# A selective scan whose tiles hold 64 channels x 2 states instead of 128 channels x 1 state

## The chip, the cores and the metric

The kernel runs on one NeuronCore of a Trainium2 chip. The metric is the device time of one execution in microseconds (us); lower is better. TensorE is called PE in the profile, VectorE DVE, ScalarE ACT, GpSimd POOL, and SP is the engine that issues most of the DMAs.

## The reference, cut to what matters

Eight images of 64 channels x 64 x 64 positions go through four layers: a self-attention over 4096 positions, two window-attention blocks with an MLP, a filter layer, and a state-space layer (SS2D) with an output stage. The change lies in the scan of the last one. It has B = 8 images, K = 4 directions, 128 channels c, N = 16 states n, and 4096 positions in a row:

```
def step(h, inp):
    u_t, dt_t, B_t, C_t = inp
    h = h * exp(dt_t[..., None] * A) + dt_t[..., None] * B_t[:, :, None, :] * u_t[..., None]
    return (h, einsum('bkcn,bkn->bkc', h, C_t))
```

So for each image, direction, channel and state there is a first-order recurrence along the positions, h = exp(dt*A[c,n])*h + (dt*u)[c]*B[n], and the output y[c] is the sum over the 16 states of h*C[n]. B and C depend on the state and the position, not on the channel; dt and u depend on the channel and not on the state; A depends on both.

## The kernel before, in words

**Frame.** The images are worked on in four pairs. First a head runs with PE alone in charge: all layers up to the scan's inputs for the first pair, and the first layer for the second. Then `scans` runs for pair after pair, 512 steps each, and feeds other work in beside the steps from generators: the front of the next pair (`front`: the attention of `layer0`, the window blocks of `layer1`, `layer2`, `scan_sources`) and the back of the pair before (`back`). The loop at the end of each step advances the generators in a fixed proportion to the steps done, so the amount of other work per step is fixed by their costs. Beside the last pair there is only back work. A second, general program at the end of the kernel is entered only when values run out of range; it isn't touched.

**A unit** is one image, one direction and one chunk of 512 positions: 64 units per pair, 256 in all. `inputs` (called one unit ahead, after the second step) loads the unit's x tile (L1703), makes dt in PSUM with a matmul (L1706), Exp and Ln on ACT (L1708, L1711), then writes dt*x (L1712, DVE) and dt (L1713, ACT) to the tile `du`. A second matmul (L1715) gives the 16 rows of B and 16 of C, ACT copies them (L1717), and SP stores them to DRAM as `rows` (L1719).

**A step** takes two of the 16 states; eight steps make a unit. `fetch` (L1726, SP) loads two rows of B, three steps ahead, and two of C, two steps ahead, each row spread over all 128 partitions: a tile of 128 x 2 x 512 floats. B and C have three buffers each. `products` (L1731, POOL, two steps ahead) makes v = B * (dt*x) for both states in one instruction; v has six buffers. `step` then does for each state j: Exp(dt*A) on ACT into a PSUM bank `dad` (L1753), the scan on DVE (L1756) into `hd` or in place into `dad`, a small ACT copy of the last column to `carry` (L1764), and the product with C. The number `own` says how many of the two states have that product on DVE (L1771) rather than on POOL (L1767 for both states at once, L1771 for one).

**The sum over states.** `sums` runs one step late: per state one matmul of v with a 128 x 128 identity (L1795) that accumulates in the PSUM bank `yd`. At the unit's end DVE adds `yd` to `Y` (L1805 to L1810).

**The dense stretches.** While `layer0` runs beside the scan it sets `dense` to 1. Then `own` is one higher, the products that DVE makes are not given to PE but added up by DVE in the tile `ysum` (L1774, L1776, L1777), and `ysum` goes through PE once per unit.

**Order.** Every engine runs its instructions in one static order. A scheduler of the language makes it from the program's order and dependencies and may interleave scan and other work; `net.behind` (in `sums`) ties a sum behind the product of the next step. All B and C loads, the x loads and the stores of `rows` sit in SP's one queue, which stops at the first DMA whose wait isn't met. PSUM has three banks for `dad`, `pdd` and `pbc` (tag da), one for `yd`, three for the other work and one for its totals.

Of the kernel before, what the change touches and what calls it, by code (L numbers as in the profile page):

```python
# [9 lines left out]
F32 = mybir.dt.float32  # L10
AF = mybir.ActivationFunctionType
ALU = mybir.AluOpType
# [3 lines left out]
B, C, HH, WW = 8, 64, 64, 64  # L16
L = HH * WW
P = 128
# [5 lines left out]
DI, NST, RNK, KDIR = 128, 16, 4, 4  # L24
TD = 512
# [63 lines left out]
def _pack(w):  # L89
    items = []  # L90

    def put(name, a):
        a = np.asarray(a, np.float32)
        shape = a.shape
        flat = a.reshape(shape[0], -1)
        if shape[0] < P:
            flat = np.concatenate([flat, np.zeros((P - shape[0], flat.shape[1]), np.float32)], axis=0)
        items.append((name, shape, flat))

    eye = np.eye(64, dtype=np.float32)  # L100
# [5 lines left out]
    f = {k[len("L0_conv_"):]: v for k, v in w.items() if k.startswith("L0_conv_")}  # L106
# [7 lines left out]
    f = {k[len("L1_conv_"):]: v for k, v in w.items() if k.startswith("L1_conv_")}  # L114
# [36 lines left out]
    f = {k[len("L2_conv_"):]: v for k, v in w.items() if k.startswith("L2_conv_")}  # L151
# [29 lines left out]
    f = {k[len("L3_conv_"):]: v for k, v in w.items() if k.startswith("L3_conv_")}  # L181
# [11 lines left out]
    put("xbc", xp[:, RNK:].transpose(2, 0, 1))  # L193
    put("xr", xp[:, :RNK].transpose(1, 0, 2))
    put("drT", f["dtproj_w"].transpose(2, 0, 1))
    put("alogs", f["A_logs"].reshape(KDIR, DI, NST).transpose(1, 0, 2))
    dtT = f["dtproj_w"].transpose(2, 0, 1)
    put("dtT", np.concatenate([np.zeros((2 * NST,) + dtT.shape[1:], np.float32), dtT], axis=0))
    put("dtb", f["dtproj_b"].T)
# [8 lines left out]
    for i in range(4):  # L208
        s = slice(16 * i, 16 * i + 16)
# [948 lines left out]
class _Direct:  # L1158
# [112 lines left out]
    def layer0(self, p):  # L1271
# [11 lines left out]
        with self.work("w0") as wk:  # L1283
# [40 lines left out]
            self.dense = 0  # L1324
            sums = net.sums[:, p]
            nc.vector.tensor_reduce(sums, parts, AX.X, ALU.add)
            rec = wk.tile([P, 2, 32], F32, name="rec", tag="rec", bufs=1)
            nc.vector.reciprocal(rec, sums)
# [368 lines left out]
    def inputs(self, u):  # L1697

        nc, w, net = self.nc, self.w, self.net
        wk, ps = self.sw, self.ps  # L1700
        k, c = u["k"], u["c"]
        x = u["x"] = wk.tile([P, TD], F32, name="xs", tag="xs")
        nc.sync.dma_start(x, self.kept[u["image"]][k % 2][:, c * TD : (c + 1) * TD])  # L1703

        pd = ps.tile([P, TD], F32, name="pdd", tag="da")
        nc.tensor.matmul(pd, lhsT=net.xdt[:, k, :], rhs=x, start=True, stop=True)  # L1706
        du = u["du"] = wk.tile([P, 2, TD], F32, name="du", tag="du")
        nc.scalar.activation(  # L1708
            pd, pd, AF.Exp, bias=w["dtb"][:, k : k + 1], accum_out=net.esum[:, u["image"], k, c : c + 1]
        )  # L1710
        nc.scalar.activation(pd, pd, AF.Ln, bias=1.0)  # L1711
        nc.vector.tensor_tensor(du[:, 1], pd, x, ALU.mult)  # L1712
        nc.scalar.activation(du[:, 0], pd, AF.Copy)  # L1713
        pb = ps.tile([2 * NST, TD], F32, name="pbc", tag="da")
        nc.tensor.matmul(pb, lhsT=w["xbc"][:, k, :], rhs=x, start=True, stop=True)  # L1715
        bc = wk.tile([2 * NST, TD], F32, name="bc", tag="bc")
        nc.scalar.activation(bc, pb, AF.Copy)  # L1717
        rows = u["rows"] = self.dram.tile([2 * NST, TD], F32, name="rows", tag="rows")
        nc.sync.dma_start(rows, bc)  # L1719

    def fetch(self, i, st, s):

        n = NST * s + 2 * (i % 8)
        t = st["BC"[s]] = self.sw.tile([P, 2, TD], F32, name="BC"[s], tag="BC"[s], bufs=3)
        row = self.units[i // 8]["rows"][n : n + 2].rearrange("r t -> (r t)")
        self.nc.sync.dma_start(t.rearrange("p r t -> p (r t)"), row.unsqueeze(0).to_broadcast([P, 2 * TD]))  # L1726

    def products(self, i, st):
        v = st["v"] = self.sw.tile([P, 2, TD], F32, name="vd", tag="v", bufs=6)
        dx = self.units[i // 8]["du"][:, 1:2]  # L1730
        self.nc.gpsimd.tensor_tensor(v, st["B"], dx.to_broadcast([P, 2, TD]), ALU.mult)  # L1731

    def step(self, i, st):

        nc, w, net = self.nc, self.w, self.net
        wk, ps = self.sw, self.ps
        u = self.units[i // 8]
        k, c, at, CC, v = u["k"], u["c"], u["at"], st["C"], st["v"]


        n0 = 2 * (i % 8)
        own = 1 + (i % 4 == 3) if u["image"] >= B - 2 else i % 2 + self.dense
        rev = k >= 2

        def along(t):
            return t[:, ::-1] if rev else t

        h = wk.tile([P, 2 - i % 2, TD], F32, name="hd", tag=f"h{i % 2}", bufs=1)
        hs = []
        for j in range(2):  # L1750
            n = n0 + j
            da = self.bank("dad", (P, TD), "da")
            nc.scalar.activation(da, u["du"][:, 0], AF.Exp, scale=net.As[:, k, n : n + 1])  # L1753
            first = 0.0 if at == 0 else self.carries[:, n : n + 1]
            to = da if j >= 2 - own else h[:, j]
            nc.vector.tensor_tensor_scan(along(to), along(da), along(v[:, j]), first, ALU.mult, ALU.add)  # L1756
            hs.append(to)
            if at < NTD - 1 and (own or j):
                ends = h[:, :, 0] if rev else h[:, :, TD - 1]
                cs = self.carries[:, n0 : n0 + 2]  # L1760
                if own:
                    ends = to[:, 0:1] if rev else to[:, TD - 1 : TD]
                    cs = self.carries[:, n : n + 1]
                nc.scalar.activation(cs, ends, AF.Copy)  # L1764

        if own == 0:
            st["w"] = nc.gpsimd.tensor_tensor(v, h, CC, ALU.mult)  # L1767
        for j in range(2 if own else 0):
            if j < 2 - own or not self.dense:
                engine = nc.vector if j >= 2 - own else nc.gpsimd  # L1770
                m = engine.tensor_tensor(v[:, j], hs[j], CC[:, j], ALU.mult)  # L1771
            elif "sum" not in u:
                s = u["sum"] = wk.tile([P, TD], F32, name="ysum", tag="ysum", bufs=1)
                m = nc.vector.tensor_tensor(s, hs[j], CC[:, j], ALU.mult)  # L1774
            else:
                m = nc.vector.tensor_tensor(hs[j], hs[j], CC[:, j], ALU.mult)  # L1776
                nc.vector.tensor_tensor(u["sum"], u["sum"], hs[j], ALU.add)  # L1777
            st.setdefault("w", m)
        st["to_y"] = [v[:, j] for j in range(2) if not self.dense or j < 2 - own]
        if i % 8 == 7 and "sum" in u:  # L1780
            st["to_y"].append(u["sum"])

    def sums(self, i, st, after=None):

        nc, w, net = self.nc, self.w, self.net
        wk, ps = self.sw, self.ps
        u = self.units[i // 8]
        k, c = u["k"], u["c"]
        srcs = st["to_y"]
        for j, v in enumerate(srcs):  # L1790
            start = "y" not in u
            if start:
                u["y"] = ps.tile([P, TD], F32, name="yd", tag="y", bufs=1)
            stop = i % 8 == 7 and j == len(srcs) - 1
            m = nc.tensor.matmul(u["y"], lhsT=w["ident"], rhs=v, start=start, stop=stop)  # L1795
            if after is not None and j == 0:
                net.behind(m, after)
        if i % 8 < 7:
            return

        y = u["y"]
        yd = net.part(self.Y, k, c)
        yp = y.rearrange("p (a b) -> p a b", b=64)
        if u["nth"] == 0:
            nc.vector.scalar_tensor_tensor(yd, self.img(u["x"]), net.dsum, yp, ALU.mult, ALU.add)  # L1805
        elif u["nth"] < 3:
            nc.vector.tensor_tensor(yd, yd, yp, ALU.add)
        else:
            o = u["x"]
            nc.vector.tensor_tensor(self.img(o), yd, yp, ALU.add)  # L1810
            nc.sync.dma_start(u["out"][:, c * TD : (c + 1) * TD], o)
# [155 lines left out]
```

## Time and profile before

| | us |
|---|---|
| median of 3 runs (13437.7 to 13443.52) | 13439.18 |
| span of the profiled execution | 13435.7 |
| of it before the first product of the scan | 2189 |
| PE busy | 10771.7 (80%) |
| DVE busy | 8806.3 (66%) |
| POOL busy | 7764.7 (58%) |
| ACT busy | 7082.9 (53%) |
| DMA: bytes moved, mean rate | 2385 MB, 178 GB/s |

The span is the time from the first to the last instruction of one profiled execution; the runs are separate, unprofiled executions. Busy times of engines overlap, so they don't add up to the span. In a group's line the columns are: source line, engine, operation, output<-inputs, shapes, count; then busy time and mean duration in ns; then idle time of the engine just before these instructions and what ended it. Each float32 matmul of the program shows as two records of PE. In the table by stage each row gives a stretch of time, its length, and for each engine the busy time and (in brackets) the number of instructions.

### The profile page before, as it was taken

How to read it: one execution, taken by the hardware profiler on the slowest of the kernel's cores; microseconds unless marked ns; L12 is line 12 of the kernel's file. 1: busy time of each engine (PE TensorE's matmuls, PEld its weight loads, DVE VectorE, ACT ScalarE, POOL GpSimd, SP SyncE). 2: the span in 40 equal slices, each digit the busy share in tenths (PEclk: the TensorE clock that was granted, in tenths of full speed). 3: DMA queues.
4: the chain of work that ended last, by engine and by line, in shares of the span. 5: the costliest groups of instructions: out<-in, count | busy, mean ns of one | idle time of the engine just before them, and what ended most of it. 6: DMA issues, size and time to landing. Idle time of an engine off the chain costs nothing. (4 is left out here: it accounts for less than half of the span.)

```text
span 13435.7 us, 140355 instructions
## 1 busy us (share of the span) xinstructions
PE 10771.7 (80%) x45762; PEld 3974.5 (30%) x45762; DVE 8806.3 (66%) x10407; ACT 7082.9 (53%) x15569; POOL 7764.7 (58%) x3875
## 2 busy tenths in 40 slices
PE   9999986888787669989888666997898766666676
PEld 2243322333232222224433222223443222222222
DVE  0121236777768676676666767667676767987987
ACT  5556514565535646655554644664654554454553
POOL 0000004888778765466666686446766677787883
PEclk9999977998898789989899788998989878888888
DMA  0000004666667765455555675445545577677884
GB/s 24 1 1 1 1 14 166 233 236 218 212 213 239 237 206 170 161 182 173 172 177 175 224 241 177 157 161 179 192 170 170 195 239 260 233 281 263 293 297 156
DMA packets 706250, 2385.13 MB, mean 178 GB/s; under 512 B 81120, under 2 KB 81248, under 8 KB 704480
## 3 DMA queue, kind: packets, MB, share of 16 engines
q1 hardware_dynamic: 681312, 2319.76, 51.0%
q10 hardware_dynamic: 24192, 56.29, 1.1%
q8 instruction: 362, 5.93, 0.2%
q14 instruction: 384, 3.15, 0.1%
HBM read 2272.97 MB, written 102.76 MB: 177 GB/s over the span
## 5 line engine op out<-in xcount | busy, mean ns | idle before, releaser
L1731 POOL TENSOR_TENSOR vd<-B,du 128x1024 f32<-128x1024 f32 x2048 | 4832.8, 2367 | 3958.5 <-DMA B<-rows 2538.2
L1795 PE MATMUL yd<-vd,pack 128*128 128x512 f32 x7540 | 4300.3, 701 | 1351.0 <-POOL vd L1767 585.1
L1753 ACT ACTIVATE dad<-du,As 128x512 f32<-128x512 f32 x4096 | 2729.4, 681 | 1136.3 <-DVE hd L1756 686.4
L1756 DVE TENSOR_TENSOR_SCAN hd<-dad,carry,vd 128x512 f32<-128x512 f32 x2166 | 2714.5, 1270 | 683.9 <-ACT dad L1753 392.9
L1795 PEld LDWEIGHTS yd<-vd,pack 128*128 128x128 f32 x7540 | 1509.5, 217 | 3824.9 <-issue 1678.9
L1767 POOL TENSOR_TENSOR vd<-hd,C 128x1024 f32<-128x1024 f32 x658 | 1551.0, 2357 | 1050.5 <-DVE hd L1756 690.5
L1756 DVE TENSOR_TENSOR_SCAN dad<-dad,carry,vd 128x512 f32<-128x512 f32 x1418 | 1791.8, 1275 | 118.9 <-ACT dad L1753 64.8
L1771 POOL TENSOR_TENSOR vd<-hd,C 128x512 f32<-128x512 f32 x1154 | 1477.9, 1281 | 522.0 <-DVE hd L1756 474.3
L1313 ACT ACTIVATE e<-s 128x512 f32<-128x512 f32 x2048 | 1200.8, 591 | 750.3 <-PE s L1307 748.7
L1307 PE MATMUL s<-X 64*128 64x512 f32 x4096 | 1343.9, 646 | 30.5 <-ACT e L1313 28.8
L1299 PE MATMUL po<-e,VT 128*64 128x512 f32 x4096 | 1227.0, 621 | 12.6 <-ACT e L1313 9.9
L1771 DVE TENSOR_TENSOR vd<-dad,C 128x512 f32<-128x512 f32 x1300 | 866.0, 673 | 67.1 <-ACT carry L1764 46.8
L1764 ACT ACTIVATE carry<-hd 128x1 f32<-128x1 f32 (+1 forms) x1586 | 316.8, 201 | 908.0 <-DVE hd L1756 904.9
L1764 ACT ACTIVATE carry<-dad 128x1 f32<-128x1 f32 x1422 | 240.5, 169 | 786.5 <-DVE dad L1756 783.6
L1307 PEld LDWEIGHTS s<-X 64*128 64x128 f32 x4096 | 375.6, 186 | 914.9 <-issue 782.8
L1447 DVE TENSOR_TENSOR w_e<-w_s,bias 128x512 f32<-128x512 f32 x512 | 330.0, 681 | 426.9 <-PE w_s L1435 426.3
L1462 PEld LDWEIGHTS w_av<-vals,w_e 64*64 64x64 f32 x16384 | 538.9, 143 | 195.4 <-issue 84.2
L1462 PE MATMUL w_av<-vals,w_e 64*64 64x9 f32 x16384 | 567.1, 206 | 32.0 <-ACT w_e L1452 31.8
L1706 PE MATMUL pdd<-xs,xdt 128*128 128x512 f32 x512 | 343.0, 757 | 236.8 <-DMA xs<-xc 102.8
L1452 ACT ACTIVATE w_e<-w_e 128x512 f32<-128x512 f32 x512 | 311.9, 626 | 367.7 <-DVE w_e L1447 250.6
L1299 PEld LDWEIGHTS po<-e,VT 128*64 128x64 f32 x4096 | 236.3, 135 | 847.2 <-issue 763.6
L1574 PE MATMUL acc<-tap,pack 128*128 128x512 f32 x576 | 367.1, 761 | 98.2 <-DVE tap L1573 96.8
(252 smaller groups left out, 11102.0 us busy)
## 6 DMA issues: line engine op xcount, KB each, us to landing
B<-rows SPq DMA_DIRECT2D x2048, 512.0 KB, 5.1
C<-rows SPq DMA_DIRECT2D x2048, 512.0 KB, 4.5
xs<-xt SPq DMA_DIRECT2D x128, 256.0 KB, 3.6
xs<-xc SPq DMA_DIRECT2D x128, 256.0 KB, 4.2
xc<-xcv ACTq DMA_DIRECT2D x64, 256.0 KB, 3.9
zs<-z ACTq DMA_DIRECT2D x64, 256.0 KB, 3.8
xt<-XT ACTq DMA_DIRECT2D x32, 512.0 KB, 7.9
rows<-bc SPq DMA_DIRECT2D x256, 64.0 KB, 1.6
```

Source lines behind the costliest of these rows:

```text
L1299: nc.tensor.matmul(po[half[im]], lhsT=VT[:, t, half[im]], rhs=es[im], start=(t == 0), stop=(t == 31))
L1307: nc.tensor.matmul(ss[im], lhsT=at(half[im], t), rhs=X[half[im], jc * CH : (jc + 1) * CH], start=True, stop=True)
L1313: nc.scalar.activation(e, ss[im], AF.Exp, scale=C**-0.5, accum_out=parts[:, im, t, jc : jc + 1])
L1462: nc.tensor.matmul(self.av[half[im], x % 4 + j, h, :], lhsT=es[h // 4][half[im], j, h % 4, :], rhs=V[half[im], x + j, h, :], start=True, s ...
L1574: nc.tensor.matmul(acc, lhsT=w["ident"], rhs=tap, start=(t == 0), stop=(t == TAPS - 1))
L1731: self.nc.gpsimd.tensor_tensor(v, st["B"], dx.to_broadcast([P, 2, TD]), ALU.mult)
L1753: nc.scalar.activation(da, u["du"][:, 0], AF.Exp, scale=net.As[:, k, n : n + 1])
L1756: nc.vector.tensor_tensor_scan(along(to), along(da), along(v[:, j]), first, ALU.mult, ALU.add)
L1764: nc.scalar.activation(cs, ends, AF.Copy)
L1767: st["w"] = nc.gpsimd.tensor_tensor(v, h, CC, ALU.mult)
L1771: m = engine.tensor_tensor(v[:, j], hs[j], CC[:, j], ALU.mult)
L1795: m = nc.tensor.matmul(u["y"], lhsT=w["ident"], rhs=v, start=start, stop=stop)
```

## The change

The tile of one scan instruction holds 64 channels x 2 states on its 128 partitions (partition 2c + s is channel c, state s of the pair), where it held 128 channels x 1 state. Per step there are still two scan tiles; the index j now means the half of the channels, and not the state.

- B and C: a load writes two rows alternately to the partitions, 128 x 512 floats (256 KB in place of 512 KB). Both halves of the channels read the same tile. The buffers are four each.
- dt and dt*x: computed as before, into a tile `du1` (one buffer). Two DMAs per unit on SP (512 KB each, SBUF to SBUF) write every channel's two rows to two neighbouring partitions of `du`, one DMA per half of the channels. Exp and the products read `du`.
- The sums: per half one matmul with `fold`, a 128 x 64 matrix with two ones in each column, so that it adds the two states of a channel; half 0 goes to partitions 0 to 63 of `yd`, half 1 to partitions 64 to 127.
- `ysum` and its DVE additions are gone; in the dense stretches all 16 tiles of a unit go through PE. `own` is as before.
- The table of A is laid out to match. The rows' copy `bc` has one buffer in place of two.

```diff
-        du = u["du"] = wk.tile([P, 2, TD], F32, name="du", tag="du")
+        one = wk.tile([P, 2, TD], F32, name="du1", tag="du1", bufs=1)
+        du = u["du"] = wk.tile([P, 2, 2, TD], F32, name="du", tag="du")
...
-        nc.vector.tensor_tensor(du[:, 1], pd, x, ALU.mult)
-        nc.scalar.activation(du[:, 0], pd, AF.Copy)
+        nc.vector.tensor_tensor(one[:, 1], pd, x, ALU.mult)
+        nc.scalar.activation(one[:, 0], pd, AF.Copy)
+        for g in range(2):
+            src = one[self.HALF[g]].rearrange("c q t -> c (q t)").unsqueeze(1).to_broadcast([64, 2, 2 * TD])
+            nc.sync.dma_start(du[:, g].rearrange("p q t -> p (q t)"), src)
...
-        bc = wk.tile([2 * NST, TD], F32, name="bc", tag="bc")
+        bc = wk.tile([2 * NST, TD], F32, name="bc", tag="bc", bufs=1)
...
-        t = st["BC"[s]] = self.sw.tile([P, 2, TD], F32, name="BC"[s], tag="BC"[s], bufs=3)
-        row = self.units[i // 8]["rows"][n : n + 2].rearrange("r t -> (r t)")
-        self.nc.sync.dma_start(t.rearrange("p r t -> p (r t)"), row.unsqueeze(0).to_broadcast([P, 2 * TD]))
+        t = st["BC"[s]] = self.sw.tile([P, TD], F32, name="BC"[s], tag="BC"[s], bufs=4)
+        row = self.units[i // 8]["rows"][n : n + 2]
+        self.nc.sync.dma_start(t, row.unsqueeze(0).to_broadcast([64, 2, TD]))
...
-        self.nc.gpsimd.tensor_tensor(v, st["B"], dx.to_broadcast([P, 2, TD]), ALU.mult)
+        self.nc.gpsimd.tensor_tensor(v, self.twice(st["B"]), self.units[i // 8]["du"][:, :, 1], ALU.mult)
...
-            nc.scalar.activation(da, u["du"][:, 0], AF.Exp, scale=net.As[:, k, n : n + 1])
+            nc.scalar.activation(da, u["du"][:, j, 0], AF.Exp, scale=net.As[:, k, n : n + 1])
...
-            if j < 2 - own or not self.dense:
-                engine = nc.vector if j >= 2 - own else nc.gpsimd
-                m = engine.tensor_tensor(v[:, j], hs[j], CC[:, j], ALU.mult)
-            elif "sum" not in u:
-                s = u["sum"] = wk.tile([P, TD], F32, name="ysum", tag="ysum", bufs=1)
-                m = nc.vector.tensor_tensor(s, hs[j], CC[:, j], ALU.mult)
-            else:
-                m = nc.vector.tensor_tensor(hs[j], hs[j], CC[:, j], ALU.mult)
-                nc.vector.tensor_tensor(u["sum"], u["sum"], hs[j], ALU.add)
+            engine = nc.vector if j >= 2 - own else nc.gpsimd
+            m = engine.tensor_tensor(v[:, j], hs[j], CC, ALU.mult)
...
-            m = nc.tensor.matmul(u["y"], lhsT=w["ident"], rhs=v, start=start, stop=stop)
+        for j in range(2):
+            m = nc.tensor.matmul(
+                u["y"][self.HALF[j]], lhsT=w["fold"], rhs=st["v"][:, j], start=(i % 8 == 0), stop=(i % 8 == 7)
+            )
```

## The prediction

> **What bounds it now.** First the slices of the page.
>
> ```profile
> PE   9999986888787669989888666997898766666676
> POOL 0000004888778765466666686446766677787883
> PEclk9999977998898789989899788998989878888888
> DMA  0000004666667765455555675445545577677884
> ```
>
> No engine is full throughout. After the head (6 slices, no scan, not touched) the limit moves, so I cut the scan at its stages and read the table of busy time (columns: stretch, its length, PE, weight loads, DVE, ACT, POOL, clock, DMA share, GB/s).
>
> ```profile
> 2189.00:3076.00 887.00, 728.70 (x4929) 324.08 (x4929) 664.28 (x754) 511.73 (x1027) 783.19 (x383) 0.92 0.70 236
> 3076.00:4236.00 1160.00, 947.91 (x3683) 376.68 (x3681) 818.60 (x907) 556.33 (x1133) 921.69 (x449) 0.90 0.64 216
> 5070.00:5880.00 810.00, 774.29 (x2368) 211.13 (x2367) 525.63 (x619) 536.62 (x1549) 365.35 (x183) 0.98 0.49 164
> 5880.00:7412.00 1532.00, 1293.03 (x8031) 579.18 (x8030) 1065.86 (x1313) 791.81 (x1525) 1006.80 (x489) 0.89 0.53 178
> 7412.00:8270.00 858.00, 547.46 (x882) 186.01 (x882) 639.79 (x690) 428.88 (x786) 618.97 (x297) 0.77 0.64 218
> 11171.00:13436.00 2265.00, 1507.36 (x2618) 499.84 (x2618) 1950.98 (x2142) 1081.97 (x2425) 1676.18 (x896) 0.85 0.74 256
> ```
>
> With the steps counted by L1731 in each: A (first row) 192 steps of 4.62 us, POOL 88%; B 224 of 5.18, PE 82%, POOL 79%; D (dense) 119 of 6.8, PE 96%; E 245 of 6.25, PE 84%; F 149 of 5.76, no engine above 75%; G (last pair) 512 of 4.42, DVE 86%. D, E and F return for the third pair (119, 245 and 97 steps); 4236 to 5070 (C, 149 steps of 5.6) is like F. POOL works about 4.1 us per step in A to F outside D.
>
> Then the groups and who keeps POOL waiting.
>
> ```profile
> L1731 POOL TENSOR_TENSOR vd<-B,du 128x1024 f32<-128x1024 f32 x2048 | 4832.8, 2367 | 3958.5 <-DMA B<-rows 2538.2
> L1795 PE MATMUL yd<-vd,pack 128*128 128x512 f32 x7540 | 4300.3, 701 | 1351.0 <-POOL vd L1767 585.1
> L1299 PE MATMUL po<-e,VT 128*64 128x512 f32 x4096 | 1227.0, 621 | 12.6 <-ACT e L1313 9.9
> ```
>
> ```profile
> POOL vd L1731 <- DMA B<-rows: 2538.2, 227, 2172.5
> POOL vd L1731 <- PE yd L1795: 769.3, 181, 19.0
> ```
>
> The sums cost PE 4300 us. POOL waits 769 us until a late sum frees a buffer of v. Of the wait for B, 2172.5 is the head; 366 us is left.
>
> **The skill.** (1) "TensorE: Matmul & The Clock Gate", section "Part 3: Packing small matmuls — row/col tiling": matmuls in different column groups run at once. The trace agrees: attention's L1299 has the shape of the new sums (128 rows, 64 columns, two halves of one bank), and a pair costs 1227.0/1024 = 1.20 us busy against 4300.3/3770 = 1.14 for one full matmul. (2) "TensorEngine Tiling (Array Packing)", "Key Properties": a change of tiling mode drains the engine. In the dense stretch a pair, a full matmul and the next pair start 1.01 and 1.05 us apart, so I take 1.20 per pair with drains in it.
>
> ```profile
> 5530.97 1.08 PE L1299 MATMUL po<-e,VT 128*64 128x512 f32 x4
> 5531.98 1.13 PE L1795 MATMUL yd<-vd,pack 128*128 128x512 f32 x2
> 5533.03 1.13 PE L1307 MATMUL s<-X 64*128 64x512 f32 x4
> ```
>
> (3) The first of these pages, "Part 1: The HAM clock gate": an idle PE falls to half its clock. The table agrees: 0.77 in F with PE at 64%, 0.98 in D. A relieved PE will be slower per matmul. (4) "SBUF — State Buffer", "Door 1: The DMA port swizzle": 64 partitions reach half of the ports. The DMAs of du read 64; no run here shows its price yet.
>
> **Part by part.**
>
> *Sums outside D.* Two matmuls (2 x 1.12 in E) become a pair of 1.20. The built order of PE has both halves adjacent for 65% of the pairs in E, about 90% in B and A, nearly all in F and G; I count a split pair at the price of two. E: 551 us of sums become 245 x (0.65 x 1.20 + 0.35 x 2.24) = 383, so 168 less. B: 485 become 292, 193 less. A: 408 become 257. What reaches the end? From A to B to E, PE work per step grows 3.80, 4.23, 5.28 and the step 4.62, 5.18, 6.25: about 1 us per us. But other work grows with it, and split stages wait on DVE and ACT too, so I take 0.6 in E: -101, twice: -202. B has POOL's floor near, A's 4.62 per step: 0.5, -97. A is on that floor: -20.
> C and both F (395 steps) hold about 1 us of PE relief per step, which nothing there is short of; 0.15 for shorter waits: -55. G is DVE's: 512 x 1.1 x 0.1 = -56, with B's waits in it.
>
> *D, the dense stretches.* PE did 88 full matmuls (176 records, 96.5 us) in 119 steps; it will do 119 pairs x 1.20 = 143. PE is the bound, so +46, twice: +92. The 100 us per stretch of ysum additions that DVE loses are hidden behind PE and bring nothing. If PE had slack the +92 would vanish.
>
> *B and C.* 4096 loads halve. The floor is the 256 KB row.
>
> ```profile
> B<-rows SPq DMA_DIRECT2D x2048, 512.0 KB, 5.1
> xs<-xt SPq DMA_DIRECT2D x128, 256.0 KB, 3.6
> ```
>
> So B lands about 1.5 us sooner; only the 366 us of waits can gain, and they are counted in the shares above. The fourth buffer takes a wait from SP (fetches wait on POOL and DVE there), with the same cover.
>
> *du.* 512 more DMAs of 512 KB on SP, 268 MB against 1074 MB saved. In SP's built order they stand right after the store of rows, ahead of the next unit's first B, and wait for the DVE product and the ACT copy. In the timelines of all units that pair ends 2.2 us (median) after bc, then two issues of 0.35. Queued behind it: the C and B fetches; who waits: POOL's first products and the first Exp of the unit. The two land at best in 5.1 + 2 = 7 us (B's row, the second overlapped), at worst in 2 x 5.1 = 10.2. Before, from the end of dt*x and dt to the first product there were 9.9 us in the median unit, 6.8 in the lower quarter, 4.8 at least; to the first Exp 16.4. So most units hide it and a quarter to a half are late by 1 to 3 us. Bounds: 0 and 256 x 2.5 = 640, since no copy over DMA can gain against reading in place. I take 0.35 us per unit: +90. If the cover goes (a faster step leaves fewer us), this cost grows.
>
> *POOL, DVE, ACT instructions* keep shape and count outside D; a repeated operand already costs nothing in L1731 (2367 ns, du repeated) against L1767 (2357, none repeated). 0; up to 1% of POOL (+80) if B's repeat is dearer.
>
> **Sum.** -202 - 97 - 20 - 55 - 56 = -430; +92 + 90 = +182; net -248. Profiled span 13435.7 - 248 = 13188; the median of the runs lies 3.5 above that span: 13191, say 13190.
>
> **Rivals.**
> - *Relief all the way* (13%): E at 1.0, B to A's floor (-125), C and F at 0.4 since POOL waits 769 us on sums, du hidden. -336 - 125 - 20 - 146 - 100 + 92 = -635: 12800. Against: F has an idle PE already and is no faster.
> - *PE's relief is covered* (12%): the clock falls and DVE/POOL chains set the pace; gains -180 against +92 + 90: 13440. For it: F's 5.76 us per step at PE 64%.
> - *du delays each unit* (20%, slower): SP stands at du and the megabyte delays B and the first Exp. It decides from (430 - 92)/256 = 1.3 us per unit on the path; at 2.5 it is +640 - 338 = +302: 13740. For it: the 4.8 us units and half the ports; against: the median cover of 9.9.
> - *The halves don't overlap* (5%): 238 full matmuls at 1.10 per dense stretch, 262 against 96.5, +165 twice, +90, -60 for B: 13800. L1299 speaks against it.
>
> **Numbers.** Forecast 50%. Faster: 50 + 13 + 3 (of the covered case) = 66%; within 0.2%, about what a measurement can tell: 7%; slower: 27%. Range 12900 to 13600: it cuts the far ends of the first and the last two rivals, about 20%.
>
> **What would show it.** yd's busy time falling from 4331 to about 2700 with pairs 1.2 us apart; D longer by 46 us; E shorter by about 100; POOL's wait for yd under 400. Wrong, if waits for du stand ahead of Exp and L1731 products, if E keeps 6.25 us per step, or if the clock falls below 0.8 where PE was the bound.

## The result and the profile after

The changed kernel takes 13271.72 us (median of 4 runs, 13267.58 to 13288.26) against 13438.44 us before (4 runs, 13408.89 to 13443.52): a ratio of 0.9874 with a 95% interval of 0.9855 to 0.9893, so 167 us or 1.3% faster. Its profiled span is 13286.5 us, 149 us less than before's 13435.7.

The slices of the page, to be laid beside the first four lines of the prediction:

```profile
PE   9999985777777567987888655997887756665566
POOL 0000003888788684456675677447566777887994
PEclk9999976777787578998888676998788867777787
DMA  0000003444445553333343454334333455665663
```

PE lost a tenth or two in many slices, and its granted clock (PEclk) fell with it. DMA lost one or two tenths nearly everywhere. POOL is about as full as it was, and at the end (the last pair) fuller.

The table of busy time, cut at the same scan units as the stages A, B, D, E, F and G (columns as in the prediction: stretch, its length, PE, weight loads, DVE, ACT, POOL, clock, DMA share, GB/s):

```profile
2201.00:3093.00 892.00, 696.03 (x4931) 270.38 (x4934) 658.47 (x752) 506.77 (x1026) 782.22 (x383) 0.77 0.50 151
3093.00:4215.00 1122.00, 858.91 (x3666) 282.81 (x3663) 817.71 (x902) 547.13 (x1124) 917.58 (x448) 0.78 0.48 144
5015.00:5924.00 909.00, 835.76 (x2894) 238.35 (x2895) 512.05 (x566) 578.66 (x1623) 410.40 (x205) 0.95 0.35 104
5924.00:7396.00 1472.00, 1177.48 (x7855) 468.84 (x7853) 1030.17 (x1280) 775.29 (x1489) 985.86 (x479) 0.84 0.39 118
7396.00:8228.00 832.00, 460.38 (x864) 104.05 (x863) 641.90 (x671) 424.76 (x776) 600.42 (x291) 0.66 0.50 151
11143.00:13286.00 2143.00, 1284.15 (x2594) 275.62 (x2592) 1933.92 (x2130) 1076.93 (x2413) 1677.88 (x896) 0.78 0.58 175
```

E has 240 steps between these unit boundaries; for before, the same units give this row:

```profile
5910.00:7412.00 1502.00, 1264.37 (x7858) 566.08 (x7857) 1045.67 (x1285) 779.72 (x1495) 990.39 (x482) 0.89 0.53 179
```

So E is 30 us shorter, with 87 us less of PE's busy time. G is 121 us shorter, the largest piece by far. The groups of the changed kernel, for the product with B, the sums, and attention's pair:

```profile
L1740 POOL TENSOR_TENSOR vd<-B,du 128x1024 f32<-128x1024 f32 x2048 | 4818.1, 2366 | 3533.2 <-DMA B<-rows 2362.5
L1791 PE MATMUL yd<-vd,pack 128*64 128x512 f32 x8192 | 3311.3, 782 | 1888.0 <-POOL vd L1776 996.9
L1301 PE MATMUL po<-e,VT 128*64 128x512 f32 x4096 | 1200.0, 621 | 5.0 <-ACT e L1315 5.0
```

The repeated B costs POOL nothing (2366 ns, 2367 before). The sums fell from 4300 us to 3311, not to some 2700. What POOL waited for (columns: who <- for whom, us in total, times, longest):

```profile
POOL vd L1740 <- DMA B<-rows: 2362.5, 64, 2184.2
POOL vd L1776 <- DVE hd L1765: 1034.3, 209, 37.7
POOL vd L1740 <- PE yd L1791: 674.6, 220, 29.9
```

Outside the head, waits for B fell from 366 to 2362.5 - 2184.2 = 178 us. The wait for a late sum fell from 769 only to 675. The wait for the scan's output rose; before, this line read:

```profile
POOL vd L1767 <- DVE hd L1756: 690.5, 179, 23.5
```

The DMAs (columns: KB each, median us from issue to landing):

```profile
B<-rows SPq DMA_DIRECT2D x2048, 256.0 KB, 3.5
du<-du SPq DMA_DIRECT2D x512, 512.0 KB, 6.1
```

A stretch of PE's timeline in D (start, us, engine and line) shows the pairs in one piece:

```profile
5469.26 1.08 PE L1301 MATMUL po<-e,VT 128*64 128x512 f32 x4
5470.17 1.03 PE L1791 MATMUL yd<-vd,pack 128*64 128x512 f32 x4
5471.13 1.13 PE L1309 MATMUL s<-X 64*128 64x512 f32 x4
```

Four records in 0.96 us: the two halves run side by side, and here, where PE is full, a pair costs what one full matmul did (1.05 us in the prediction's lines).

### The profile page after: what moved, and what is told of

Its sections match the earlier page's. It is cut to its first block, busy times and chain, and to the rows that moved or that the text cites. A ratio compares the mean times of both kernels' runs of the same rounds, so it can differ in the third digit from the quotient of the medians.

```text
span 13286.5 us, 142109 instructions
## 1 busy us (share of the span) xinstructions
PE 10111.5 (76%) x46358; PEld 3219.0 (24%) x46358; DVE 8619.6 (65%) x10109; ACT 7086.1 (53%) x15584; POOL 7760.7 (58%) x3875
## 5 line engine op out<-in xcount | busy, mean ns | idle before, releaser
L1740 POOL TENSOR_TENSOR vd<-B,du 128x1024 f32<-128x1024 f32 x2048 | 4818.1, 2366 | 3533.2 <-DMA B<-rows 2362.5
L1791 PE MATMUL yd<-vd,pack 128*64 128x512 f32 x8192 | 3311.3, 782 | 1888.0 <-POOL vd L1776 996.9
L1791 PEld LDWEIGHTS yd<-vd,pack 128*64 128x64 f32 x8192 | 661.3, 162 | 4084.1 <-POOL vd L1776 1472.5
L1301 PE MATMUL po<-e,VT 128*64 128x512 f32 x4096 | 1200.0, 621 | 5.0 <-ACT e L1315 5.0
L1779 DVE TENSOR_TENSOR vd<-dad,C 128x512 f32<-128x512 f32 x1626 | 1078.5, 676 | 49.4 <-ACT carry L1773 47.2
L1464 PEld LDWEIGHTS w_av<-vals,w_e 64*64 64x64 f32 x16384 | 614.3, 159 | 240.2 <-issue 110.4
L1464 PE MATMUL w_av<-vals,w_e 64*64 64x9 f32 x16384 | 643.4, 216 | 24.6 <-ACT w_e L1454 24.4
L1708 PE MATMUL pdd<-xs,xdt 128*128 128x512 f32 x512 | 397.0, 867 | 276.2 <-DMA xs<-xc 101.6
L1765 DVE TENSOR_TENSOR_SCAN hd<-dad,vd 128x512 f32<-128x512 f32 x304 | 362.8, 1212 | 168.6 <-POOL vd L1776 67.8
```

The costliest lines, as they stand in the source:

```text
L1301: nc.tensor.matmul(po[half[im]], lhsT=VT[:, t, half[im]], rhs=es[im], start=(t == 0), stop=(t == 31))
L1464: nc.tensor.matmul(self.av[half[im], x % 4 + j, h, :], lhsT=es[h // 4][half[im], j, h % 4, :], rhs=V[half[im], x + j, h, :], start=True, s ...
L1740: self.nc.gpsimd.tensor_tensor(v, self.twice(st["B"]), self.units[i // 8]["du"][:, :, 1], ALU.mult)
L1779: m = engine.tensor_tensor(v[:, j], hs[j], CC, ALU.mult)
L1791: m = nc.tensor.matmul(u["y"][self.HALF[j]], lhsT=w["fold"], rhs=st["v"][:, j], start=(i % 8 == 0), stop=(i % 8 == 7))
```

## The experiments

The stages of each kernel were cut at the same scan units; each figure is the stage's length minus before's in the profiled execution, in us (F2 is the shorter F of the third pair; what precedes A is left out). The columns are, from the left: the changed kernel; its pairs made twice; no copies of du; the kernel before with half loads in four and in three buffers; the changed kernel with three buffers; the kernel before with half loads and the fold, and with the fold alone; the sums on DVE again; five buffers for B and C.

```
stage steps before | after pairs no    half, half, after, half+ before dense after,
                   |       twice du    4 buf 3 buf 3 buf  fold  fold   sums  buf 5,
                   |                                                          v 5
A     192    887   |   +5   +32   +15   +13   +26   +17   +15   +39   +12    +9
B     224   1161   |  -38   +30   -13   +13   +25   -22    -3   -57   -22   -23
C     144    810   |  -11   +10   -10    -6    +6   -10    -9   +12    -6    -4
D     128    864   |  +45   +30   +41   +24   +26   +49   +35    +4   +21   +48
E     240   1502   |  -30   +46   -19    -8   +12   -16   -17    +9   -16    -8
F     144    838   |   -6   +13   -11    -2    +9   -15    +5   -16    -8   -14
D2    128    865   |   +3   +12    +3    -1     0   +22    -3    +1    +9   +18
E2    240   1504   |  -23   +35   -28    -2    -1   -12   -18    -6   -23   -10
F2     96    552   |  +14    +2   +25    +7   +18   +14   +19    -6   +14   +11
G     512   2265   | -121   -56  -121  -110   -89   -77  -116   +17   -75  -145
```

A single stage moves by 10 to 30 us from build to build without a cause that I can name, so the text leans on totals of repeated runs and on stages that move together. The interval of a difference between two kernels is worked out from the intervals of their ratios to before (the root of the sum of squares, times 13440 us).

The theory when these began: PE's relief (the pairs) makes the gain. The rival: the halved loads of B and C make it.

**Pairs made twice.** The changed kernel with each pair outside the dense stretches made a second time, so that PE does the work of before and the sum y comes out double there.

```diff
...
+        for j in range(0 if st["dense"] else 2):
+            nc.tensor.matmul(
+                u["y"][self.HALF[j]], lhsT=w["fold"], rhs=st["v"][:, j], start=False, stop=(i % 8 == 7)
+            )
```

> The changed kernel, but outside the dense stretches each pair of half-column sums is made twice (so y is wrong there: its sum over states counts double). PE's sums cost about 2 x 1.15 us per step again, as before the change; the halved loads, the du DMAs and the dense stretches stay. Theory P (the gain of 167 us is PE's relief): the gain is gone, 13400 or more, with the last pair's stretch back at 2260 us from 2144. Theory L (the gain is the halved B and C loads, PE had slack and lost clock to it): 13260 to 13310, the last stretch within 30 us of 2144.

13588.0 us, ratio 1.0116 (1.0089 to 1.0142): 325 ± 44 us slower than the changed kernel by the ratios. The gain is gone, as the first theory expected, but G gave back only 65 of its 121 us. PE's work is not wholly covered when it is added: over the scan the doubled pairs add 964 us to PE's busy time (8096 to 9060), of which a third shows. Doubling is no clean undoing, though: sums in E took 589 us here against 540 before, and the next runs say what taking work away brings.

**No copies of du.** The two DMAs of each unit are left out, and Exp and the products read the tile of 128 channels, that is, the wrong channels.

```diff
...
-        for g in range(2):
-            src = one[self.HALF[g]].rearrange("c q t -> c (q t)").unsqueeze(1).to_broadcast([64, 2, 2 * TD])
-            nc.sync.dma_start(du[:, g].rearrange("p q t -> p (q t)"), src)
```

> The changed kernel without the two du DMAs per unit: Exp and the products read the undoubled tile in place, so dt and dt*x are those of the wrong channels, everything else is as in the change. If the du DMAs cost what the prediction took (0.35 us per unit, 90 us): 13180. If they are hidden by the cover of about 10 us per unit: 13250 to 13280. If they are worse than taken (over 1 us per unit): below 13000.

13315.6 us, ratio 0.9911 (0.9889 to 0.9932): outside all three expectations, and not faster than with the copies, rather 50 ± 39 us slower, for which I have no cause. The copies cost nothing that their removal gives back.

**Half loads alone.** The kernel before with loads of 256 KB and four buffers; half of the channels then read the wrong row.

```diff
-        t = st["BC"[s]] = self.sw.tile([P, 2, TD], F32, name="BC"[s], tag="BC"[s], bufs=3)
+        t = st["BC"[s]] = self.sw.tile([P, TD], F32, name="BC"[s], tag="BC"[s], bufs=4)
...
+        self.nc.sync.dma_start(t, row.unsqueeze(0).to_broadcast([64, 2, TD]))
```

> The kernel before with loads of 256 KB in four buffers as in the change, full-column sums, ysum and du in place as before; both states of a tile then read rows that are mixed over the partitions, so the values are wrong. Theory L: at least half of the gain, 13280 to 13350, most of it in the last pair's stretch (DMA share 0.74 there). Theory P: within 30 us of 13438.

13372.21 us, ratio 0.995 (0.9934 to 0.9967): -67 us, outside both expectations, less than half of the change's gain. G is 110 us shorter, and there are small losses elsewhere.

**The fold alone.** The kernel before with one pair of half-column sums in place of the two full sums, outside the dense stretches; it adds neighbouring channels, which are not the states of one channel.

```diff
...
+            if len(srcs) == 2:
+                m = nc.tensor.matmul(u["y"][self.HALF[j]], lhsT=w["fold"], rhs=v, start=start, stop=stop)
```

> The kernel before with half-column pairs (fold) in place of the two identity matmuls outside the dense stretches; loads, du and ysum as before; it adds neighbouring channels, so y is wrong. Theory P: the whole gain and more, since the dense stretches keep their DVE sums and there are no du DMAs: 13180 to 13270. Theory L: 13400 to 13440.

13433.47 us, ratio 0.9992 (0.9979 to 1.0004): nothing. Yet the fold took 572 us from PE's busy time over the scan (8765 to 8193). Neither theory holds alone: loads bring 67, the fold 11 ± 17, together less than 167. The edit to the loads had two parts, though, the size and the number of buffers, and the prediction had set the second at nothing. The next four runs part them.

**Three buffers in the changed kernel.**

```diff
-        t = st["BC"[s]] = self.sw.tile([P, TD], F32, name="BC"[s], tag="BC"[s], bufs=4)
+        t = st["BC"[s]] = self.sw.tile([P, TD], F32, name="BC"[s], tag="BC"[s], bufs=3)
```

> The changed kernel with three buffers for each of B and C instead of four, nothing else. If the gain of the last pair comes from the smaller loads themselves, 13230 to 13320 us, and the last pair is within 40 us of the changed kernel's 2144 us. If it comes from the fourth buffer (a load that can be issued a step earlier), 13350 to 13420 us, and the last pair is back near the 2265 us of before.

13383.51 us, ratio 0.9959 (0.9945 to 0.9973): 114 ± 32 us lost with the fourth buffer. G lost 44 of it; the rest is spread over most stages.

**Half loads, three buffers, in the kernel before.**

```diff
-        t = st["BC"[s]] = self.sw.tile([P, TD], F32, name="BC"[s], tag="BC"[s], bufs=4)
+        t = st["BC"[s]] = self.sw.tile([P, TD], F32, name="BC"[s], tag="BC"[s], bufs=3)
```

(against the half loads above)

> The kernel before with loads of 256 KB for B and C instead of 512 KB, in three buffers as before (half of the channels read the wrong one of the two rows). If the size of the loads made the gain that the version with four buffers showed (last pair 110 us shorter), the last pair is 80 to 120 us shorter here as well and the whole 13340 to 13390 us; if the fourth buffer made it, the last pair is within 25 us of before and the whole 13420 to 13460 us.

13466.98 us, ratio 1.0018 (1.0011 to 1.0025): the smaller loads alone make the kernel 24 ± 9 us slower. Both expectations miss. G is 89 us shorter, as if the size made G's gain, but the stages before it are longer by 121 in all. The waits of POOL in this kernel:

```profile
POOL vd L1735 <- DMA B<-rows: 2209.2, 14, 2173.6
POOL vd L1771 <- DVE hd L1760: 1117.5, 228, 17.1
```

Of the 366 us of waits for B, 36 are left, and the wait for the scan's output is 427 us longer (1117.5 against 690.5). The wait moved to another partner of POOL; the whole did not get shorter.

The four times make a square, and within the intervals its two effects add:

| | three buffers | four buffers | fourth buffer |
|---|---|---|---|
| scan tiles of before, loads of 256 KB | 13466.98 | 13372.21 | -91 ± 25 |
| tiles of the change, loads of 256 KB | 13383.51 | 13271.72 | -114 ± 32 |
| new tiles and sums | -79 ± 21 | -102 ± 34 | |

(Differences are from the ratios.) From before to after: +24 for the size, -91 for the buffer, -102 for the new tiles and sums. That these make up the whole difference (-169 by the ratios) is so by construction; what is measured is that the buffer is worth about as much with either kind of tile (91 and 114). Where the buffer acts is seen in SP's own waits, first of the changed kernel with three buffers, then with four (the load at the head of SP's queue stands until POOL's product frees a buffer):

```profile
SPq L1732 <- POOL vd L1740: 2848.4, 1370, 22.5
```

```profile
SPq L1732 <- POOL vd L1740: 1934.8, 989, 25.9
```

The same in the kernel before with half loads, three buffers and four:

```profile
SPq L1726 <- POOL vd L1735: 3175.6, 1527, 14.5
```

```profile
SPq L1726 <- POOL vd L1735: 2401.0, 1217, 16.0
```

SP stands 775 to 914 us less in this line; its waits for the products with C rise, and all that a load of B or C waits for falls by 403 us in the kernel before (6297 to 5893) and by 517 in the changed one (5635 to 5118). By which waits of the compute engines that becomes 91 to 114 us I cannot follow. In the changed kernel POOL's waits for C fall from 78 us to 13 and its waits for the scan by 41; in the kernel before its waits for the scan fall by 146; the rest is spread thin.

One rival is not tested. With a fourth buffer the language's scheduler also puts SP's queue in another order: in the changed kernel 3352 of SP's 5414 DMAs stand where another kind of DMA stood with three buffers, while on POOL 158 of 3884 instructions do. It also lets loads go out earlier: with four buffers 708 of the 2048 loads of B were issued while three earlier products of POOL had still to begin, with three buffers none was. The smaller loads in three buffers changed SP's order as well (2457 of 4902 DMAs). So "the fourth buffer" here means the buffer together with the order that comes with it; no run holds one of them fixed.

**Each load twice.** The changed kernel with three buffers, and a second load of the same rows into a tile that nothing reads, one such tile for B and one for C.

```diff
+        again = self.sw.tile([P, TD], F32, name="again", tag="again" + "BC"[s], bufs=1)
+        self.nc.sync.dma_start(again, row.unsqueeze(0).to_broadcast([64, 2, TD]))
```

> The changed kernel with three buffers, and after each load of B or C a second one of the same 256 KB into a tile that nothing reads: the queue moves as many bytes again as in the kernel before, but each step waits only for its first half. If the bytes on the queue are what counts, the gain of the last pair (121 us) is gone and the whole is 13370 to 13430 us; if it is the time to landing of the load that is waited for, 13250 to 13320 us.

14104.28 us, ratio 1.0496 (1.048 to 1.0512): outside both expectations, because of a wait that I had put in myself:

```profile
SPq L1734 <- DMA again<-rows: 2634.5, 2560, 4.4
```

The idle tile has one buffer, so a second load stands on SP until the one before has landed, 1.0 us on average, 2560 times, and the real loads stand behind it. The page "DMA: Bandwidth & Descriptors", section "Anatomy of one DMA — SWDGE (gpsimd) path", of the Trainium skill says that a DMA's semaphore wait is spent on the issuing sequencer, before dispatch; this queue shows it. On bytes against landing the run decides nothing. The kernel is 720 us slower than with three buffers alone, with 2634 us of standing added, and outside the head POOL's waits for B rise from 157 us to 915. That fits a high price of time at the head of SP's queue, but doesn't show it by itself: the real loads also land later here (B in 4.3 us, 3.2 with three buffers alone).

**Sums on DVE again in the dense stretches**, one per half, with three buffers for B and C to make room.

```diff
...
+            elif s is None:
+                s = u["sum", j] = wk.tile([P, TD], F32, name="ysum", tag=f"ysum{j}", bufs=1)
+                m = nc.vector.tensor_tensor(s, hs[j], CC, ALU.mult)
+            else:
+                m = nc.vector.tensor_tensor(hs[j], hs[j], CC, ALU.mult)
+                nc.vector.tensor_tensor(s, s, hs[j], ALU.add)
```

> The changed kernel, with VectorE's additions back in the three dense stretches (one sum per half, one pair per unit for those halves, as before the change) and three buffers instead of four for B and C to make room; to be read against the run with three buffers alone. If TensorE's time sets the dense stretches, each of the first two is some 40 us shorter than there, and the whole 80 to 100 us shorter. If VectorE's relief paid for TensorE's added pairs there, each stays within 15 us and the whole within 30 us of that run.

13349.6 us, ratio 0.9939 (0.9924 to 0.9954), 27 ± 28 us less than with three buffers alone. D is 28 us shorter and D2 13, between the two expectations. D of the run with three buffers alone, then of this one:

```profile
5027.00:5940.00 913.00, 839.16 (x2894) 238.31 (x2895) 512.91 (x567) 579.44 (x1624) 410.97 (x206) 0.95 0.34 104
```

```profile
5028.00:5913.00 885.00, 807.76 (x2622) 227.46 (x2624) 594.73 (x702) 579.20 (x1623) 408.25 (x205) 0.96 0.35 107
```

With the sums on DVE, PE is busy for 31 us less and the stretch 28 us shorter, while DVE does 82 us more. That fits PE setting the pace of D, but 28 us is within what a stage moves from build to build; the last kernel below repeats it (D 26 us and D2 10 shorter than in the change). PE's busy time changed by 31 us where the time of the sums alone differs by 55 (151 against 96 us): PE's other matmuls took up the difference.

**Half loads, four buffers, and the fold**, on the kernel before: the two edits shown above together.

> The kernel before with loads of 256 KB in four buffers and, outside the dense stretches, the pair of half-column sums (wrong rows and neighbouring channels added: the output is not the reference's). The same with full sums took 13372, the changed kernel 13272. If the 100 us between them come from TensorE's relief outside the dense stretches, this one takes 13250 to 13300 us; if TensorE's relief is worth nothing here either, as it was with loads of 512 KB, 13350 to 13390 us, and the 100 us belong to the dense stretches and the new tiling of the scan.

13318.02 us, ratio 0.9906 (0.9892 to 0.992): 59 ± 29 us less than without the fold, again between the two expectations. With large loads and three buffers the fold brought 11 ± 17. That the fold is worth more with small loads and four buffers is likely (48 ± 34), not shown beyond doubt. Rows for A and E without the fold, then with it:

```profile
2191.00:3091.00 900.00, 745.88 (x4921) 330.30 (x4920) 660.42 (x749) 507.10 (x1024) 778.93 (x381) 0.90 0.37 121
5956.00:7449.00 1493.00, 1249.47 (x7857) 560.99 (x7856) 1041.83 (x1285) 778.56 (x1495) 989.78 (x480) 0.90 0.29 96
```

```profile
2186.00:3088.00 902.00, 705.07 (x4921) 270.58 (x4920) 654.28 (x749) 505.26 (x1024) 778.40 (x381) 0.76 0.37 121
5945.00:7430.00 1485.00, 1183.55 (x7859) 468.77 (x7858) 1038.96 (x1285) 777.93 (x1495) 989.81 (x482) 0.83 0.29 96
```

In E the sums take 143 us less (528 to 385), PE's busy time falls by 66, and the stage by 8. In A 122 us of sums go (418 to 296), PE is relieved by 41, and the stage does not move. Meanwhile PE's other matmuls, the same in number, are busy for 62 us more in E (767 to 829) and 80 more in A (351 to 431). The clock falls from 0.90 to 0.83 and to 0.76; an estimate by the clock alone gives 767 x 0.90/0.83 = 832 and 351 x 0.90/0.76 = 416. So the slower clock eats about half of the saving.

**Five buffers for B and C, five for v instead of six.**

```diff
-        v = st["v"] = self.sw.tile([P, 2, TD], F32, name="vd", tag="v", bufs=6)
+        v = st["v"] = self.sw.tile([P, 2, TD], F32, name="vd", tag="v", bufs=5)
```

(and `bufs=5` for B and C)

> The changed kernel with five buffers for each of B and C instead of four, and five for v instead of six to make room. The fourth buffer was worth some 100 us. If what counts is how many steps ahead a load can be issued, a fifth brings another 30 to 80 us (13190 to 13240 us), unless the lost buffer of v costs it; if the fourth was enough to cover a landing of 3.5 us, 13260 to 13310 us; above 13340 us the sixth buffer of v is what POOL needs.

13335.06 us, ratio 0.9927 (0.9914 to 0.994): 71 ± 31 us slower than the change, between the second expectation and the third. G is the shortest of all (-145), but most other stages are longer, and POOL waits more for late sums (675 us with six buffers of v):

```profile
POOL vd L1740 <- PE yd L1791: 800.7, 248, 28.5
```

The fifth buffer and the lost one of v were not parted. Two attempts to spend the room better: sums on DVE for the second half only, with four buffers for B and three for C:

> The changed kernel with VectorE's additions back in the dense stretches for the second half of the products alone, four buffers for B and three for C. If the additions are worth some 15 to 20 us of each of the two dense stretches that I measure, as the version with both sums and three buffers showed, and the buffers of B count more than those of C, 13230 to 13290 us; if both need four, 13310 to 13360 us.

13370.38 us, ratio 0.9948 (0.9936 to 0.9961): above both expectations, and not clearly better than three buffers for both. And sums on DVE for both halves, with four buffers for B and C and five for v:

> The changed kernel with VectorE's additions back in the dense stretches for both halves, four buffers each for B and C, and five for v instead of six. If the sixth buffer of v is worth little, the 34 us that these additions brought with three buffers come here too: 13220 to 13260 us. If POOL needs it, 13290 us or more.

13282.35 us, ratio 0.9885 (0.987 to 0.9899): between the two expectations, and 15 ± 32 us from the change. No version here is clearly faster than the change.

## Why the prediction was right or wrong, point by point

The direction and the order of size hold (-248 forecast, -167 measured, inside the range), but the sum comes out near by luck in good part: terms with opposite errors met. Of the four signs that the prediction named, one came (D 45 us longer); E is 30 us shorter and not 100, POOL's wait for yd is 675 us and not under 400, and yd's busy time is 3311 and not 2700. Two of its signs of being wrong came near or came true: E took 6.13 us per step (6.25 named), and the clock in B, where PE was the fullest engine, fell to 0.78 (0.8 named).

- *The price of the sums in E* was right: 383 us forecast for 245 steps, 382 measured for 240. In B (292 against 337) and A (257 forecast, 250 by its own shares, against 297) it was low; the clock fell to 0.78 and 0.77 there, and the forecast kept the old price of 1.20. Most was missed in C, both F and G, where the table has the least PE work: 1606 us for 896 steps, 1.79 each, where 1.20 makes 1075. These 531 us are most of the 611 by which 3311 exceeds 2700. PE's clock is 0.64 to 0.78 in these stages, and a pair that starts after idle time takes up to 1.98 us (lines at the end). So in G the relief was 0.5 us per step (1174.6 to 914.5 us for 512), and not 1.1.
- *The share that reaches the end* is the step that failed: "I take 0.6 in E: -101, twice: -202". E and E2 got 30 and 23 us shorter, B 38 where 97 stood, and C with both F together 3 where 55 stood, though these figures have the fourth buffer's part in them. It failed twice over. First, the saving of the sums was taken as PE's relief: with the fold added to half loads, E's sums lose 143 us and PE only 66, mostly because the other matmuls slow down with the clock. Second, of the relief itself little is on the path: over the scan the fold took 579 us from PE's busy time (8748 to 8169) and 59 ± 29 us from the kernel's with half loads, and 572 and 11 ± 17 us without: a tenth and a fiftieth. The prediction named the falling clock, from the skill, and even made it a sign of error, but put no number on it. The slope it used ("about 1 us per us") compares stages that differ in more than PE's work. It doesn't hold for added work either: the doubled pairs cost a third of what they add to PE's busy time (325 of 964 us).
- *The fourth buffer* was the largest error: "The fourth buffer takes a wait from SP ..., with the same cover" and so nothing. With the order of SP's queue that comes with it, it is worth 91 to 114 us, over half of the whole gain. That SP's fetches wait for POOL and DVE for some 6500 us stood in SP's waits of before, and SP's queue also carries x, rows and du. A wait of SP was taken as covered because no compute engine's line names it. Its two largest lines for the loads, before:

```profile
SPq L1726 <- POOL vd L1767: 2180.4, 626, 24.4
SPq L1726 <- DVE vd L1771: 1735.4, 849, 11.8
```

- *B and C half as large*: B lands in 3.5 us instead of 5.1, 1.6 sooner where 1.5 was forecast. "Only the 366 us of waits can gain" was right as a bound, and too kind: alone the size, with the changed order of SP's queue, costs 24 us, and POOL's wait moves to the scan. G is the exception, 89 us shorter by the size alone, where the forecast had 56 for everything in G and 121 came.
- *The dense stretches*: +92 forecast. Between kernels with equal loads and buffers (the change against half loads; both with three buffers) D grows by 21 and 23 us and D2 by 4 and 22, so 25 to 45 in all. The pairs' price was near (112 us of sums in D became 150), but PE's other matmuls took less: in the run with DVE's sums back, 55 us of sums are 31 us of PE. That the additions which DVE loses bring nothing fits the same run: adding 82 us of them to D did no visible harm.
- *du*: +90 forecast, nothing found. A copy lands 6.1 us after its issue, and in the timelines of all units the pair has landed 7.1 us (median) after the first was issued, which is the forecast's best case of 7. The cover did not go: the first product came 2.2 us or more after the landing in three units of four, and the instructions that read du stood 32 us for them in all, 24 times. The page "SBUF — State Buffer", section "Door 1: The DMA port swizzle", lets one fear half the rate for 64 partitions. The copies of 512 KB took 6.1 us against 5.1 for before's loads of 512 KB to 128 partitions, so no factor of two is seen; but those loads come from DRAM, so this is no clean comparison.
- *The instructions of POOL, DVE and ACT*: 0, as forecast (2366 ns against 2367).
- *The rivals*: "PE's relief is covered" describes most stages correctly, and without the fourth buffer the time (13384 us) comes within 60 us of its 13440. The slower rival, du on the path, did not come; the halves do overlap.

What stays open: which part of the new tiling brings the 43 us between the change and the kernel of before with half loads, four buffers and the fold (13271.72 against 13318.02; 43 ± 32 by the ratios); why the kernel without copies is not faster than with them; and whether the fourth buffer's gain comes from its depth or from the new order of SP's queue.

## What to carry to other kernels

When an edit frees room for one more buffer of a loaded tile, look at the waits of the queue that issues the loads, not only at the waits of the engines that read it, and try it: here it made more (91 to 114 us) than the relief of the busiest engine did (11 to 59). Here work taken from PE brought a tenth of its busy time or less, and work added cost a third; ask what the other matmuls will take at the lower clock before counting a saving. And vary size and number of buffers apart before believing in either, and look whether the order of the queue moved with them.

## What was not expected of the hardware

- A pair of 128 x 64 sums takes 0.86 us from start to start when pairs follow one another (pairs made twice, G), and 0.96 to 1.01 among attention's matmuls of other shapes. The difference, 0.10 to 0.15 us, is an estimate of what the change of shape costs. After 6 us of idle time the same pair takes about twice as long (first line).

```profile
12306.13 1.98 PE L1792 MATMUL yd<-vd,pack 128*64 128x512 f32 x4 [6.03 <-POOL vd L1780]
12310.36 1.02 PE L1802 MATMUL yd<-vd,pack 128*64 128x512 f32 x4
12311.22 1.02 PE L1792 MATMUL yd<-vd,pack 128*64 128x512 f32 x4
```

- The granted clock answered a small relief strongly: as PE went from 83% busy to 78% in A, it fell from 0.90 to 0.76. The page "TensorE: Matmul & The Clock Gate", section "Part 1: The HAM clock gate", says that idleness throttles and activity releases; the trace agrees, and adds how much of a saving that can eat.
